# A four-layer graph-attention stack: the second projection of layer 1 as a Strassen product over two graphs, with the instruction order taken from a run of the plan

## The chip, the cores and the metric

The kernel runs on one core of a Trainium2 chip, in fp32. The metric is the device time of one execution in microseconds, given as the median of several runs. The engines are PE (matmul; PEld is its weight load), DVE (vector), ACT (scalar functions), POOL (GpSimd) and SP, which here only issues DMAs.

## The reference, cut to what matters

There are 128 graphs of 128 nodes with 512 features each and an integer adjacency matrix. Four attention layers follow each other, each inside `x = layernorm(x + layer(x, adj))`.

```python
# x: [128, 128, 512], adj: [128, 128, 128]
# layer 0: one head, no projection
# layer 1: two GAT layers, 4 heads of 256 and then one head of 512
h = elu(gat_layer(x, mask, W1, att_src1, att_dst1, b1, concat=True))   # W1: 512 x 1024
h = gat_layer(h, mask, W2, att_src2, att_dst2, b2, concat=False)       # W2: 1024 x 512
#   gat_layer: xl = x @ W; scores from xl @ a_src, xl @ a_dst; leaky_relu, mask, softmax over sources;
#   out = attn^T @ xl, plus bias
# layer 2: 8 heads of 64, projection 512 -> 512
# layer 3: scores from a projection to 32; softmax; out = elu(attn @ x)
```

The product that changes is `h @ W2`: for each graph a 128x1024 matrix times a 1024x512 matrix.

## The kernel before, in words

The function `graph(g)` (L373) lists the operations of one graph without running anything. Each entry is an `Op` (L56): its engine, an estimated duration, a closure that emits the instructions, and the buffers that it reads and writes. All 128 graphs have the same list.

The class `Pipeline` (L67) sets the order. `plan` (L71) places the list of one graph on a circular time table of `PERIOD` = 24.9 us: every operation gets a start time such that no two operations on an engine overlap modulo the period, with an assumed `LATENCY` (L30) from each engine to a reader on another one. Random shifts (`SEED`, `SPREAD`, L34) vary the priorities. `run` (L124) then starts graph g at g times the period, sorts all operations of all graphs and of the setup by these times, gives each new buffer the first slot of its kind that is free by then, and emits them in that order. Every engine works through its own queue in this fixed order; what lies between the engines are semaphores.

A graph's chain goes as follows. `x` and `adj` are loaded (L539, L540), POOL makes the masks (L546), and the scores of layer 0 are two multiply-and-sum instructions on DVE (L557). `spread` (L385) turns a column of scores into a row that lies on all partitions: a 32x32 block transposition on DVE (L389), a small DMA to device memory (L392) and a broadcast DMA back (L396). `attend` (L437) does the leaky ReLU on ACT (L446), a masked minimum on DVE with two SBUF operands (L454), the exponential on ACT (L463) and a reciprocal (L471). `turned` (L402) transposes: blocks of 32 on DVE (L407), a DMA out (L412) and a rearranging DMA in (L422, or L417 where the result is the moving operand). `mixed` (L527) multiplies the attention weights with the values (L530). `norm` (L478) is the layer norm, with the statistics on DVE, the root on POOL and the scaling on DVE or ACT.

`project` (L509) does all three projections, with its matmuls in L515: a chunk of at most 273 columns accumulates in one PSUM bank over the 128-row pieces of the weight, and ACT (L522) or DVE (L520) evicts it. For the product in question, the stationary operand is `hT` (a graph's hidden state transposed, 8 pieces of 128x128), the moving one is `w2a`, the weight with one score column for each half (2 x 257 columns):

```python
project(hT, lambda k, c: w2a[:, k, c, :], KH, C2, xl2, ["DVE", "ACT"])   # 2 chunks x 8 matmuls
```

POOL adds the bias of layer 1 (L603), the residual's bias (L585), and the residuals of layers 2 and 3 (L671, L704), each over 512 columns at a time.

The setup loads the weights by DMA, mostly from POOL's queue (`weights`, L211), and row vectors by broadcast DMAs onto 128 partitions (`rows`, L219, and `passing`, L222). It forms extra weight columns with `dot` (L276), `dot2` (L306) and `dots` (L326), and constants with a few matmuls (`ones_out`, L294; `shifts`, L318). These steps have times of their own, written by hand, and stand in the same sorted list, but their durations and dependences aren't part of the plan.

Of the kernel before, what the change touches and what calls it, by code (L numbers as in the profile page):

```python
# [3 lines left out]

# [6 lines left out]
F32 = mybir.dt.float32  # L11
# [5 lines left out]
P = 128  # L17
# [10 lines left out]
PERIOD = 24.9  # L28
LATENCY = {"PE": (0.0, 0.8), "DVE": (0.15, 1.4), "ACT": (0.1, 1.4), "POOL": (0.1, 1.4), "SP": (6.0, 6.0)}
URGENCY = 1.0  # L30
BANKS = 8

SEED, SPREAD = 17, 3.0
# [22 lines left out]
class Op:  # L56
    def __init__(self, engine, cost, emit, ins, outs, extra):
        self.engine, self.cost, self.emit, self.extra = engine, cost, emit, extra
        self.ins, self.outs = ins, outs
        self.bufs = list(dict.fromkeys([*ins, *outs]))  # L60

    def done(self, reader=None):
        own, other = LATENCY[self.engine]
        return self.cost + self.extra + (own if reader is self.engine else other)


class Pipeline:  # L67
# [3 lines left out]
    def plan(self, ops):  # L71
# [28 lines left out]
        while waiting:  # L100
# [16 lines left out]
            for q in after[k]:  # L117
                ready[q] = max(ready[q], t + op.done(ops[q].engine))
                missing[q] -= 1
                if not missing[q]:  # L120
                    waiting.append(q)
        return times

    def run(self, setup):  # L124
        times, until = self.plan(self.make(0)), {}
        graphs = [self.make(g) for g in range(self.n)]
        for k, op in enumerate(graphs[0]):
            for b in op.bufs:
                until[b] = max(until.get(b, 0.0), times[k] + op.done())
        names = list(until)  # L130
        events = [(t, -1, k, (emit, bufs)) for k, (t, emit, bufs) in enumerate(setup)]
        free = {}
        for g, ops in enumerate(graphs):
            alive = dict(zip(dict.fromkeys(b for op in ops for b in op.bufs), names))
            for k, op in enumerate(ops):
                events.append((g * PERIOD + times[k], g, k, op))
                op.ends = [(b, g * PERIOD + until[alive[b]]) for b in op.outs]
        for t, g, k, op in sorted(events, key=lambda e: e[:3]):
            emit, ends = op if g < 0 else (op.emit, op.ends)
            for b, end in ends:  # L140
                if b.slot is None:
                    slots = free.setdefault(b.tag, [])
                    b.slot = next((s for s, e in enumerate(slots) if e <= t), len(slots))
                    assert b.tag != "ps" or b.slot < BANKS, "too few banks"
                    slots[b.slot : b.slot + 1] = [end]
                    b.ap = self.place(b, g)
            emit()
# [3 lines left out]
def tile_gat_stack(  # L151
# [53 lines left out]

    setup = []

    def at(t, emit, bufs=()):
        setup.append((t, emit, bufs))

    def weights(t, shape, name, *loads, step=0.0, by=nc.gpsimd):  # L211


        tl = const.tile(shape, F32, name=name)
        for n, (part, src) in enumerate(loads):
            at(t + n * step, lambda part=part, src=src: by.dma_start(out=part(tl), in_=src))
        return tl

    def rows(t, ap, n, name, by=nc.gpsimd):  # L219
        return weights(t, [P, n], name, (lambda w: w, ap.partition_broadcast(P)), by=by)  # L220

    def passing(t, until, n, src=None):  # L222

        b = Buf("setup", [P, n])
        load = lambda: nc.gpsimd.dma_start(out=b.ap[: src.shape[0]], in_=src)
        at(t, load if src is not None else lambda: None, [(b, until)])
        return b
# [8 lines left out]
    C1, C2, CH = FH + 2, F // 2 + 1, FO + 2  # L236
    SH = H2 * CH
    C3 = SH + 2 * H2 + 2
    flat = "h f -> (h f)"
    w0d = rows(-20, w0_dst, F, "w0d", nc.scalar)  # L240
    w0s = rows(-20, w0_src, F, "w0s", nc.scalar)
    b0t = rows(-20, b0, 1, "b0t", nc.scalar)

    w1a = weights(-19, [P, KF, H1, C1], "w1a", *(
        (lambda w, b=b, k=k: w[b::4, k, :, :FH],
         w1.rearrange("(k b a) (h c) -> b k a h c", b=4, a=32, h=H1)[b, k])
        for k in range(KF) for b in range(4)
    ))
    a1 = [passing(-18, 90, HF, a.rearrange(flat).partition_broadcast(P)) for a in (a1_src, a1_dst)]
    b1t = rows(10, b1, HF, "b1t")  # L250
    b2t = rows(16, b2, F, "b2t")
    w2a = weights(18, [P, KH, 2, C2], "w2a", *(
        (lambda w, k=k: w[:, k, :, : F // 2], w2[k * P : (k + 1) * P].rearrange("p (s c) -> p s c", s=2))
        for k in range(KH)
    ))
    a2 = [passing(20, 130, F, a.rearrange(flat).partition_broadcast(P)) for a in (a2_src, a2_dst)]
    a3 = [passing(60, 230, F, a.rearrange(flat).partition_broadcast(P)) for a in (ah2, ah1)]
    fc = passing(60, 230, F, w_fc)
    ac = weights(60, [OUT, 2], "ac", *(
        (lambda w, s=s: w[:, s : s + 1], w_attn[0:1, s * OUT : (s + 1) * OUT].rearrange("u o -> o u"))  # L260
        for s in range(2)
    ))
    wha = weights(70, [P, KF, C3], "wha", *(
        (lambda w, b=b, k=k: w[b::4, k, :SH].rearrange("p (h o) -> p h o", h=H2)[:, :, :FO],
         wh.rearrange("h (k b a) o -> b k a h o", b=4, a=32)[b, k])
        for k in range(KF) for b in range(4)
    ), step=4, by=nc.sync)
    acb = [passing(140, 230, P) for _ in range(2)]
    fcp = passing(140, 230, F)
    wf = [passing(140, 230, F) for _ in range(2)]  # L270
    prod = [passing(-20, 230, F) for _ in range(2)]
    shift2 = const.tile([P, 2], F32, name="shift2")
    swf = const.tile([P, 2], F32, name="swf")
    turn = [0]

    def dot(w, a, out):  # L276

        turn[0] ^= 1
        nc.vector.tensor_tensor_reduce(
            out=prod[turn[0]].ap[:, : a.shape[1]], in0=w, in1=a, scale=1.0, scalar=0.0, op0=ALU.mult,  # L280
            op1=ALU.add, accum_out=out,
        )

    for k in range(KF):
        for s in range(2):
            for h in range(H1):
                at((31, 33, 56, 58)[k] + s + h / 4, lambda k=k, s=s, h=h: dot(
                    w1a[:, k, h, :FH], a1[s].ap[:, h * FH : (h + 1) * FH], w1a[:, k, h, FH + s : FH + s + 1]
                ))


    at(30, lambda: nc.vector.tensor_scalar_add(b1t, b1t, 1.0))

    def ones_out(s):  # L294
        pf = psum.tile([P, 512], F32, tag=f"ps{6 + s}", name=f"pc_{s}")
        for k in range(KH):
            nc.tensor.matmul(  # L297
                pf[:, : F // 2], lhsT=minus, rhs=w2a[:, k, s, : F // 2], start=(k == 0), stop=(k == KH - 1)
            )
        cols = slice(s * F // 2, (s + 1) * F // 2)  # L300
        nc.vector.tensor_add(b2t[:, cols], b2t[:, cols], pf[:, : F // 2])

    for s in range(2):
        at(44 + s, lambda s=s: ones_out(s))

    def dot2(k, s):  # L306
        turn[0] ^= 1
        nc.vector.tensor_tensor_reduce(
            out=prod[turn[0]].ap.rearrange("p (s c) -> p s c", s=2), in0=w2a[:, k, :, : F // 2],
            in1=a2[s].ap.rearrange("p (s c) -> p s c", s=2), scale=1.0, scalar=0.0, op0=ALU.mult,  # L310
            op1=ALU.add, accum_out=w2a[:, k, s, F // 2 : C2],
        )

    for k in range(KH):
        for s in range(2):
            at(100 + 3 * k + 1.5 * s, lambda k=k, s=s: dot2(k, s))

    def shifts():  # L318
        pf = psum.tile([P, 512], F32, tag="ps7", name="pc_2")
        for k in range(KH):  # L320
            nc.tensor.matmul(pf[:, :2], lhsT=minus, rhs=w2a[:, k, :, F // 2], start=(k == 0), stop=(k == KH - 1))
        nc.vector.tensor_copy(shift2, pf[:, :2])

    at(126, shifts)

    def dots(k, a, cols):  # L326

        turn[0] ^= 1
        pr = prod[turn[0]].ap.rearrange("p (h o) -> p h o", h=H2)
        nc.vector.tensor_mul(  # L330
            pr, wha[:, k, :SH].rearrange("p (h o) -> p h o", h=H2)[:, :, :FO],
            a.ap.rearrange("p (h o) -> p h o", h=H2),
        )
        nc.vector.tensor_reduce(out=wha[:, k, cols], in_=pr, op=ALU.add, axis=AX.X)

    def columns(s):

        nc.vector.tensor_copy(acb[s].ap[:OUT], ac[:, s : s + 1].to_broadcast([OUT, P]))
        pf = psum.tile([P, 512], F32, tag="ps7", name=f"pf_{s}")
# [15 lines left out]
    for s in range(2):  # L355
        at(142 + 3 * s, lambda s=s: columns(s))
# [389 lines left out]
```

## Time and profile before

| what | value |
|---|---|
| median of 3 runs | 3253.45 us (3248.8 to 3255.87) |
| the profiled execution | 3255.44 us, span 3253.7 us |
| mean granted TensorE clock | 0.977 |
| PE, DVE busy over the span | 3113.7 us, 2862.7 us |
| ACT, POOL busy over the span | 2143.7 us, 1906.0 us |
| DMA | 601.07 MB, mean 185 GB/s |

The busy times are sums over the whole span; the table of stretches tells how they lie in the beginning, the middle and the end. In a group by line, the columns are: line, engine, operation, output and input names (buffer numbers left out), shapes and count; then the group's busy time in us and the mean of one instruction in ns; then the engine's idle time just before them and who ended it. A matmul in fp32 shows as two records. Buffers that share one size have one name, `w`, so groups are told apart by line.

### The profile page before, as it was taken

What the parts mean: (1) busy time and instruction counts of PE and PEld (TensorE: products, weight loads), DVE (VectorE), ACT (ScalarE), POOL (GpSimd) and SP (SyncE); (2) the same over time, 40 slices, a digit from 0 to 9 for tenths busy, and PEclk for the clock granted to TensorE, in tenths of its full rate; (3) what the DMA queues carried; (4) which work ended last, traced back from release to release, by engine and by line L of the source; (5) the groups of instructions that cost most, each with busy time, mean ns of one, the idle gap of its engine ahead of it and who ended that gap; (6) DMA issues with size and microseconds to landing.
All of it is one profiled execution on the core that took longest, in us unless ns stands there. A gap on an engine that the chain in (4) does not pass through costs nothing.

```text
span 3253.7 us, 61851 instructions
## 1 busy us (share of the span) xinstructions
PE 3113.7 (96%) x15292; PEld 2582.4 (79%) x15292; DVE 2862.7 (88%) x10005; ACT 2143.7 (66%) x7297; POOL 1906.0 (59%) x2985
## 2 busy tenths in 40 slices
PE   4799999999999999999999999999999999999973
PEld 2578888888888888888888888888888888888852
DVE  4678999999999999999999999999999999999875
ACT  1246676766767667677676767667676676776664
POOL 5344566656666566665666666566665666656434
PEclk8899999999999999999999999999999999999985
DMA  5257778878777777777777787777777777787764
GB/s 147 79 135 180 195 187 202 193 183 207 188 198 192 193 198 187 201 189 197 196 191 198 185 204 192 191 198 187 200 191 194 197 188 199 190 199 194 171 168 105
DMA packets 1639736, 601.07 MB, mean 185 GB/s; under 512 B 1309696, under 2 KB 1489920, under 8 KB 1639376
## 3 DMA queue, kind: packets, MB, share of 16 engines
q1 hardware_dynamic: 1636608, 589.44, 73.8%
q0 software_dynamic: 2336, 7.15, 0.7%
q8 instruction: 123, 2.02, 0.3%
q14 instruction: 237, 1.94, 0.2%
q10 hardware_dynamic: 432, 0.52, 0.1%
HBM read 369.43 MB, written 227.48 MB: 183 GB/s over the span
## 4 chain that ended last, share of the span: by engine, by line
PE 93%; DVE 3%; DMA 2%; issue 1%; POOL 1%; ACT 0%; SPq 0%; POOLq 0%; DVEq 0%; ACTq 0%
PE ps L515 69%; PE ps L530 10%; PE ps L619 7%; PE ps L659 6%; DVE w L454 1%; DMA w<-row 1%; DMA w<-scr 0%; PE ps L568 0%; DVE w L407 0%; DVE st L481 0%; PE pc L297 0%; DMA w2a<-in_L_gnn_W_dram 0%; DMA w1a<-in_L_gnn_W_dram 0%; DVE w L700 0%; DVE w L557 0%
## 5 line engine op out<-in xcount | busy, mean ns | idle before, releaser
L463 ACT ACTIVATE w<-w,nm 128x128 f32<-128x128 f32 x1920 | 749.3, 392 | 432.7 <-DVE nm L454 432.7
L515 PE MATMUL ps<-w2a,w 128*128 128x257 f32 x4096 | 968.7, 384 | 10.3 <-DVE w L569 9.1
L515 PE MATMUL ps<-w1a,w 128*128 128x258 f32 x4096 | 917.6, 382 | 0.3 <-DMA w<-scr 0.3
L515 PEld LDWEIGHTS ps<-w1a,w 128*128 128x128 f32 x4096 | 779.1, 190 | 173.2 <-issue 59.5
L454 DVE CUSTOM_DVE_ANT_0 w<-w,w 128x128 f32<-128x128 f32 x1920 | 852.2, 563 | 14.2 <-ACT w L446 13.9
L515 PEld LDWEIGHTS ps<-w2a,w 128*128 128x128 f32 x4096 | 762.7, 191 | 116.1 <-DVE w L569 9.9
L522 ACT COPY xl<-ps 128x258 f32<-128x258 f32 (+2 forms) x768 | 289.7, 377 | 409.1 <-PE ps L515 393.8
L407 DVE STREAM_TRANSPOSE w<-w 128x512 f32<-128x512 f32 (+1 forms) x1024 | 547.8, 547 | 9.8 <-ACT w L463 3.0
L446 ACT ACTIVATE w<-w,xl 128x128 f32<-128x128 f32 x1536 | 474.2, 391 | 88.4 <-DMA w<-row 68.5
L515 PE MATMUL ps<-wha,w 128*128 128x273 f32 x2048 | 511.1, 396 | 13.9 <-DMA w<-scr 13.9
L515 PEld LDWEIGHTS ps<-wha,w 128*128 128x128 f32 x2048 | 381.2, 191 | 151.9 <-issue 40.8
L500 ACT ACTIVATE w<-w,mr,rd 128x512 f32<-128x512 f32 x384 | 309.0, 807 | 89.3 <-POOL mr L493 81.4
L463 ACT ACTIVATION_READ_ACCUMULATOR w<-w,nm 128x1 f32 x1920 | 362.1, 189 | 0.0
L481 DVE BATCH_NORM_STATS2 st<-w 128x6 f32<-128x512 f32 x512 | 345.0, 674 | 9.1 <-POOL w L704 2.8
L704 POOL TENSOR_TENSOR w<-w,w 128x512 f32<-128x512 f32 x128 | 163.0, 1274 | 316.6 <-DVE w L700 316.6
L486 POOL TENSOR_TENSOR rd<-rd,neghalf 128x1 f32<-128x1 f32 x512 | 322.8, 630 | 42.6
L659 PEld LDWEIGHTS ps<-xl,w 128*128 128x128 f32 x2048 | 273.7, 195 | 88.6 <-issue 69.2
L603 POOL TENSOR_TENSOR xl<-xl,b1t 128x512 f32<-128x512 f32 x256 | 312.6, 1241 | 0.0
L485 POOL TENSOR_SCALAR rd<-mv 128x1 f32<-128x1 f32 x512 | 115.9, 226 | 332.4 <-DVE mv L482 304.0
L530 PE MATMUL ps<-w,w 128*128 128x512 f32 x512 | 278.3, 626 | 26.9 <-DMA w<-scr 9.9
L671 POOL TENSOR_TENSOR w<-z,w 128x512 f32<-128x512 f32 x128 | 151.4, 1183 | 243.6 <-PE ps L515 135.8
L454 DVE DVE_READ_ACCUMULATOR2_ANT nm<- 128x1 f32 x1920 | 292.3, 152 | 0.0
(98 smaller groups left out, 3900.4 us busy)
## 6 DMA issues: line engine op xcount, KB each, us to landing
scr<-w SPq DMA_DIRECT2D x640, 256.0 KB
w<-scr SPq DMA_DIRECT2D x640, 256.0 KB
w<-row SPq DMA_DIRECT2D x128, 512.0 KB
w<-in_x_dram SPq DMA_DIRECT2D x128, 256.0 KB
w<-row SPq DMA_DIRECT2D x128, 256.0 KB
out_dram<-w SPq DMA_DIRECT2D x128, 256.0 KB
w<-row SPq DMA_DIRECT2D x384, 64.0 KB
scr<-w SPq DMA_DIRECT2D x384, 64.0 KB
```

Of the source, the lines that this page charges most:

```text
L407: op("DVE", 0.12 + 0.133 * n, lambda: nc.vector.transpose(zb.ap.rearrange("p b h c -> p h b c"), src.ap.rearrange("p (h b c) -> p h b c", ...
L446: nc.scalar.activation(z.ap[:, h, :], db.ap[:, h0 + h, :], AF.Prelu, bias=src(h0 + h), alpha=SLOPE)
L454: nc.vector.tensor_tensor_reduce(out=zz.ap[:, h, :].rearrange("p (b a) -> p a b", b=4), in0=z.ap[:, h, :].rearrange("p (a b) -> p a b", b= ...
L463: nc.scalar.activation(zz.ap[:, h, :], zz.ap[:, h, :], AF.Exp, bias=nm.ap[:, h : h + 1], scale=-1.0, accum_out=rs.ap[:, h : h + 1],)
L481: op("DVE", 0.6, lambda: nc.vector.bn_stats(st.ap, y.ap), [y], [st])
L486: nc.gpsimd.tensor_tensor(out=rd.ap, in0=rd.ap, in1=neghalf, op=ALU.pow)
L500: op("ACT", 0.6, lambda: nc.scalar.activation(y.ap, y.ap, AF.Identity, bias=mr.ap, scale=rd.ap), [y, rd, mr], [y])
L515: op("PE", w * 4 / 2400 + 0.006, lambda k=k: nc.tensor.matmul(px.ap[:, :w], lhsT=lhs.ap[:, k, :], rhs=wa(k, c), start=(k == 0), stop=(k == ...
L522: op("ACT", 0.06 + w / 1200, lambda: nc.scalar.copy(dst(), px.ap[:, :w]), [px], [t])
L530: op("PE", width * 4 / 2400, lambda: nc.tensor.matmul(pa.ap[:, :width] if len(xv.shape) == 2 else pa.ap.rearrange("p (s c) -> p s c", s=2) ...
L603: op("POOL", 1.3, lambda h=h: nc.gpsimd.tensor_add(xl.ap[:, h : h + 2, :FH], xl.ap[:, h : h + 2, :FH], b1t[:, h * FH : (h + 2) * FH].rearr ...
L659: op("PE", 0.225, lambda u=u, h=h: nc.tensor.matmul(pa.ap[:, u * CH : (u + 1) * CH], lhsT=pt.ap[:, u, :], rhs=xl3.ap[:, h * CH : (h + 1) * ...
```

## The change

Three things change at once.

**The product over two graphs.** `hT @ W2` of graphs 2n and 2n+1 is one product of 2 x 2 blocks: the rows are the two graphs, the inner dimension is split into two halves of 512, the columns into two halves of 257. A Strassen product (in Winograd's form) needs seven block products in place of eight. The weight `w2s` holds seven blocks: four of the weight and three formed once in the setup from differences. The new function `halves` lists the operations. For an odd graph it forms two sums of `hT` blocks on POOL, and multiplies four of the products; in the following graph's list come the other three, with two more sums. The partial results are kept by accumulating further products into the same PSUM bank, by copies to SBUF on ACT (`taken`) and by additions of PSUM and SBUF on DVE (`added`). The plan knows one averaged list (`graph(None)`), in which the part after the product waits two periods (`op.wait`); a last list for g = 128 carries only the second part of the last pair.

**The order.** `plan` still gives times, now for `PERIOD` 28.0 and longer latencies. A new `order` goes through all operations with one clock for each engine and shorter latencies (`FLOW`): it always takes the operation that could start first, among those whose planned time is at most `AHEAD` = 30 us beyond the earliest one not yet issued, and gives out buffer slots as they come free in this run. The number of slots still comes from the plan.

**The loads as operations.** The setup's steps are `Op`s with durations, inputs and outputs, so `order` places them too. Row vectors are loaded as one row, and a matmul with ones spreads them (`spread_row`). The first weight comes from the ACT and SP queues in eight DMAs of each, the second from POOL's queue in four.

Besides, the mask of layer 3 is no longer kept from the start: the adjacency is loaded again in the third part. A graph's list is split into `first`, `second`, `halves` and `third`, which otherwise hold what was there.

```diff
-PERIOD = 24.9
-LATENCY = {"PE": (0.0, 0.8), "DVE": (0.15, 1.4), "ACT": (0.1, 1.4), "POOL": (0.1, 1.4), "SP": (6.0, 6.0)}
-URGENCY = 1.0
+PERIOD = 28.0
+LATENCY = {"PE": (0.0, 0.8), "DVE": (0.15, 1.6), "ACT": (0.1, 1.6), "POOL": (0.1, 1.6), "SP": (6.8, 6.8)}
+FLOW = {"PE": (0.0, 0.6), "DVE": (0.15, 0.9), "ACT": (0.1, 0.9), "POOL": (0.1, 0.9), "SP": (4.5, 4.5)}
+AHEAD = 30.0
+URGENCY = 0.3
...
-SEED, SPREAD = 17, 3.0
+SEED, SPREAD = 1, 8.0
...
+    def order(self, events):
...
+        while len(out) < n:
+            best = None
+            for e, waiting in known.items():
+                found = None
+                for i in waiting:
+                    if events[i][0] > events[low][0] + AHEAD and i != low:
+                        break
+                    t = start(i)
+                    if t is not None and (found is None or t < found[0]):
+                        found = (t, i)
+                        if t <= clock[e]:
+                            break
+                if found and (best is None or found < best):
+                    best = found
...
+    def spread_row(t, r, a):
+
+        b = passing(512, "ps")
+        at(t, "PE", 0.86, lambda: nc.tensor.matmul(
+            b.ap, lhsT=ones[0:1, :], rhs=r.ap[0:1, a : a + 512], start=True, stop=True
+        ), [r], [b])
+        return b
...
+    at(109, "POOL", 2.5, lambda: nc.gpsimd.tensor_sub(w2s[:, 5], w2s[:, 2], w2s[:, 3]), [summed_up], [t3])
+    at(109.1, "DVE", 1.1, lambda: nc.vector.tensor_sub(w2s[:, 3], w2s[:, 3], w2s[:, 0]), [summed_up, t3], [t1])
+    at(109.2, "DVE", 1.1, lambda: nc.vector.tensor_sub(w2s[:, 4], w2s[:, 2], w2s[:, 3]), [t1], [t2])
+    at(109.3, "DVE", 1.1, lambda: nc.vector.tensor_sub(w2s[:, 6], w2s[:, 1], w2s[:, 4]), [t2], [t4])
...
-        xl2 = Buf("xl2", [P, 2, C2])
-        project(hT, lambda k, c: w2a[:, k, c, :], KH, C2, xl2, ["DVE", "ACT"])
...
+            a11, a12, a21, a22 = (part(h, a) for h in ("h0", "h1") for a in range(2))
+            do((0, 1), "POOL", 1.27, {
+                1: summed(ALU.add, "s1", a21, a22), 0: summed(ALU.subtract, "s3", a11, a21), None: None
+            }, {"t": ["h1"], 1: ["h1"], 0: ["h0", "h1"]}, {"t": ["s1"], 1: ["s1"], 0: ["s3"]})
+            do((0, 1), "POOL", 1.27, {
+                1: summed(ALU.subtract, "s2", whole("s1"), a11), 0: summed(ALU.subtract, "s4", a12, whole("s2")), None: None
+            }, {"t": ["h1", "s1"], 1: ["s1", "h0"], 0: ["h0", "s2"]}, {"t": ["s2"], 1: ["s2"], 0: ["s4"]})
...
+            product((1,), ("h1", "q1"), {1: ("pa", "h0", a11, 0, True)})
+            taken((1,), ("q1", "t1"), {1: ("pa", "t1")})
+            product((0, 1), ("s1", "q2"), {1: ("pc", "h0", a12, 1, True), 0: ("pa", "s3", whole("s3"), 5, False)})
+            added((0, 1), ("q2", "t1"), {1: ("pc", "t1", "xl0", 0), 0: ("pa", "v", "xl1", 1)})
+            taken((0,), ("q2", "u3"), {0: ("pa", "u3")})
+            product((0, 1), ("s2", "q3"), {1: ("pb", "s1", whole("s1"), 3, True), 0: ("pb", "s4", whole("s4"), 2, False)})
+            taken((1,), ("q3", "v"), {1: ("pb", "v")})
+            added((0,), ("q3",), {0: ("pb", "u2", "xl0", 1)})
+            product((0, 1), ("s2", "q4"), {1: ("pa", "s2", whole("s2"), 4, False), 0: ("pd", "h1", a22, 6, True)})
+            taken((1,), ("q4", "u2"), {1: ("pa", "u2")})
+            added((0,), ("q4", "u3"), {0: ("pd", "u3", "xl1", 0)})
...
+            at, m3 = Buf("adj", [P, P], I32), Buf("m3", [P, P])
+            op("SP", 0.4, lambda: nc.sync.dma_start(out=at.ap, in_=adj[g]), [z3], [at], 1.0)
+            mask(m3, at, ALU.is_equal)
```

In `product`, each name stands for four matmuls of 128x257 over the four pieces of its operand, accumulating in the named bank; the number is the block of `w2s`, and the last entry tells whether the bank starts anew.

## The prediction

> **What bounds the kernel now.** I read three views in this order: the busy times by engine, the table of stretches, and the groups by line for the middle of the run. The first says which engine could be the bound, the second where it is.
>
> ```profile
> PE 3113.7 (96%) x15292; PEld 2582.4 (79%) x15292; DVE 2862.7 (88%) x10005; ACT 2143.7 (66%) x7297; POOL 1906.0 (59%) x2985
> ```
> ```profile
> core 0: us, PE busy (x) PEld busy (x) DVE busy (x) ACT busy (x) POOL busy (x), PEclk, DMA share, GB/s
> ...
> 20.00:40.00 20.00, 10.80 (x35) 8.35 (x35) 10.69 (x45) 0.40 (x1) 7.07 (x10) 1.00 0.51 167
> 40.00:60.00 20.00, 7.85 (x22) 5.36 (x23) 13.67 (x55) 1.39 (x5) 8.52 (x14) 0.66 0.39 99
> ...
> 1000.00:2000.00 1000.00, 1000.00 (x4993) 835.31 (x4992) 920.52 (x3233) 701.61 (x2393) 616.26 (x966) 1.00 0.79 194
> ```
> In the stretch from 1000 to 2000 us PE has no gap at all: 1000 of 1000 us busy, at full clock. DVE is at 92%, ACT 70%, POOL 62%. The chain of waits has PE on 93% of the span. One group with one record for each graph (the 128x257 eviction) appears 42 times, and the chain repeats the same piece every 23.84 us (1495.88, 1519.72, 1543.56), so a graph costs 23.84 us there. All the 140 us in which PE is idle lie before 200 us (71) and after 3000 us (69). So the middle is bound by PE, the ends by the latency of a graph's own chain.
>
> ```profile
> L515 PE MATMUL ps<-w2a,w 128*128 128x257 f32 x1344 | 314.5, 381 | 0.0
> L520 DVE COPY xl<-ps 128x257 f32<-128x257 f32 x42 | 16.9, 403 | 0.0
> L663 DVE TENSOR_TENSOR z<-ps,ri 128x264 f32<-128x264 f32 x84 | 35.4, 421 | 0.0
> L454 DVE CUSTOM_DVE_ANT_0 w<-w,w 128x128 f32<-128x128 f32 x630 | 284.6, 572 | 0.0
> L603 POOL TENSOR_TENSOR xl<-xl,b1t 128x512 f32<-128x512 f32 x84 | 102.6, 1241 | 0.0
> ```
> The first row is the product that changes: 32 records a graph (two for each of its 16 matmuls), 314.5 / 42 = 7.49 us. The fourth has a mean of 572 ns although its median over the run is 381. The order of time shows why:
>
> ```profile
> 1498.85 2.44 POOL L603 TENSOR_TENSOR xl<-xl,b1t 128x512 f32<-128x512 f32 x2
> 1499.01 1.34 DVE L454 CUSTOM_DVE_ANT_0 w<-w,w 128x128 f32<-128x128 f32 x1
> ...
> 1500.20 1.34 DVE L454 CUSTOM_DVE_ANT_0 w<-w,w 128x128 f32<-128x128 f32 x1
> ...
> 1501.39 0.38 DVE L454 CUSTOM_DVE_ANT_0 w<-w,w 128x128 f32<-128x128 f32 x1
> ```
> A masked minimum takes 1.34 us while a POOL addition of 512 columns runs, and 0.38 when it is over: 0.96 us lost each time. Over the stretch that is 630 x (0.572 - 0.381) = 120 us, or 2.87 us a graph (three such hits). Without them DVE needs (920.5 - 120) / 42 = 19.06 us a graph.
>
> **What the skill says.** The Trainium skill's "SBUF — State Buffer", section "SBUF: two separate sides", says that GpSimd and a DVE instruction with two SBUF inputs take one shared port pair as an exclusive lock for the whole instruction. The trace agrees: L454 has two SBUF inputs and waits out L603. Its "Perfetto Trace Analysis", section "Identifying the Most-Contended Engine", warns that busy matmul time is a poor measure and asks for weight-load time as well; that is 84% here, so I trust "PE bound" from the missing gaps, not from the 96%. Its "DMA: Bandwidth & Descriptors", section "Issuing engines are not separate DMA queues", says that DMAs of all engines share the same 16 and only issue time is saved by another queue; no run here shows it yet.
>
> **The change part by part.**
>
> *The product.* Sixteen matmuls a graph become 28 for two graphs. The listing of instructions shows 1792 in the new product line and 3072 in the other projections, against 5120 before in one line: 256 fewer. At 2 x 234 ns each (314.5 us / 1344 = 234 ns a record) that is 0.94 us a graph, so PE needs 22.90 us. In the fully busy stretch, 200 to 3040 us, there are 2840 / 23.84 = 119 graphs: **-111 us**. The remaining nine graphs' saving falls where PE waits anyway, and I count it at nothing.
>
> *DVE.* One 257-column copy a graph (0.40 us) becomes two additions of PSUM and SBUF; the nearest row is the 264-column product, 0.42 us. That is +0.44, so 19.50 us a graph before blocking.
>
> *POOL.* Four 512-column additions for two graphs, at 1.24 to 1.28 us (L603, L704): +2.5 us a graph, 14.7 becomes 17.2 of 22.9. POOL's own time is hidden; what it costs is the lock. In the new order, each graph's eight masked minima of layer 2 (DVE) stand right behind the ELU, while POOL's queue has there the last addition of layer 3 and then an operand sum, with nothing between but short instructions. I expect one or two hits of up to 1 us there. The two bias additions come directly behind the layer-2 residual now, while DVE has some 4 us of statistics, transposes and scaling to do, so their two hits should mostly go. I put the blocked time at 3.3 us a graph (between 2 and 5.8: two and six hits of 0.96 among eight large POOL operations, for three of six now). DVE then needs 22.8 us, 0.1 below PE.
>
> *ACT.* The 257-column eviction (375 ns) goes from one to two a graph: 17.1 of 22.9 us. The work beside it hides that; it is on the path only once per pair, through PSUM bank reuse.
>
> *PSUM.* Two banks of the pair stay occupied from one graph into the next, and their copies have to end before accumulation goes on in the same bank. The matmuls that stand between (other projections and head products, several us) cover a copy of 0.4 us. If DVE falls behind, this cover is what goes first.
>
> *SP and the DMAs.* The adjacency is loaded a second time, for layer 3, so its mask needn't be held: +128 DMAs of 64 KB, 8.4 on 589 MB. The SP queue's entries from 1499.4 to 1523.2 us add up to 20.2 of 23.8 us; with one more (0.3 to 0.7) it is 20.7 of 22.9, 90%. The DMA share goes from 79% to about 79 x 1.014 x 23.84 / 22.9 = 83%. One place is tighter: the layer-2 writes of the transposed heads and their reads now stand five rows apart on SP for many graphs, where ten stood before, so SP waits for the landing there and queues the loads behind it. Hidden as long as SP doesn't reach 100%.
>
> *The order.* The plan's times are run through per-engine queues, and an operation may be put up to 30 us ahead. The stretch that has no gap can't gain from it. The price is between zero and some tenths of a us a graph: with PE at 22.9 and DVE at 22.8 in one fixed order, any lateness of DVE shows as a bubble on PE. I take 0.15 x 119 = **+18 us** (0 to 0.5, so 0 to 60).
>
> *Head.* Row vectors come as 2 to 4 KB and are spread by 13 matmuls (about 1 us each, into idle PE) in place of about 3.3 MB of broadcast DMAs. In the head above, the first operand transposition left at 21.5 us and the first large matmul of layer 1 began at 54.5, with three DMA round trips of 7 to 9 us in between beside that traffic. One graph more may start early. But the third layer starts two periods later, so PE has less to do. I take **-10** (-40 to +20).
>
> *Tail.* Once the last hidden state is there, two sums (2.5 us) and 20 of the pair's 28 matmuls are left, 9.4 us against 7.5 for 16; that is 4.4 more, and with a hop between engines **+5** (0 to 15). After that, two graphs do layer 2 side by side rather than one after the other, at no cost, since from 3140 us on PE is idle over half.
>
> *Sum.* The profiled execution took 3255.4 us (span 3253.7), 2 above the median 3253.45. 3255.4 - 111 + 18 - 10 + 5 = 3157; less 2, **3155 us** as the median.
>
> **The rivals.**
>
> *DVE becomes the bound, mildly.* For it: 92% busy already, and 22.8 against 22.9 is within my error. Against: it needs blocked time over 3.4 us. At 3.9 a graph costs 23.4, a saving of 0.44 x 119 = 52; with head and tail about 3197.
>
> *The port lock takes it all back (slower).* Every added POOL sum meets a two-input DVE instruction, and the later work on DVE meets more of the old ones. It decides from 23.84 - 19.50 = 4.34 us of blocked time a graph. With six hits it is 5.8, a graph costs 25.3, and the time is 3255 + 1.46 x 119 = about 3425. For it: POOL rises from 62% to 75% busy. Against: PE, not DVE, sets the pace now, and the two structural hits go.
>
> *SP or the DMAs become late (slower).* If the waits of write-then-read add 3.5 us to SP's 20.7, a graph costs 24.2: +43, about 3300. Against: nine rows or more stand between most pairs, as now.
>
> *The ends gain more.* If starting graphs early and the missing broadcasts fill 40 us of the 71 in the head, and PE shows no bubbles, the time is 3255 - 111 - 40 = about 3105.
>
> *The change doesn't save what it says.* The listing has the 256 matmuls gone, of one shape; this one has no share.
>
> **How the numbers follow.** A measurement here can tell 0.2%, 6.5 us, from no change. The main case (3120 to 3185) has 0.43, the mild DVE bound 0.22, the good ends 0.13: together 0.78 faster. Within 0.2% falls 0.05, between the mild case and the two rivals on the other side. Slower has 0.17: the lock 0.12, SP 0.05. The range, 3098 to 3265, takes in the three fast cases and the near edge of those two.
>
> **What would show it.** Right: PE still without gaps in the middle, a period near 23.05 us, DVE at 97 to 99%, the masked minimum's mean still near 600 ns, POOL near 75%. Wrong: a period above 23.3 with DVE at 100% and a masked mean above 650 ns (the lock); PE waiting for DMA landings with SP full (the queue); or PE idle of over 150 us at the ends. A period of 22.9 with no idle would say that my bubble was invented.

## The result, and the profile after

The changed kernel takes 3279.78 us (median of 5 runs, 3269.54 to 3289.32), 1.0081 times the time before, with a 95% interval of 1.0055 to 1.0107. It is slower by 0.8%; 3155 us was forecast. Its profiled execution took 3273.89 us, with a span of 3272.1.

First the busy times by engine, then the stretch from 1000 to 2000 us, both of the kernel after:

```profile
PE 3072.9 (94%) x14822; PEld 2483.6 (76%) x14822; DVE 2939.1 (90%) x10185; ACT 2157.7 (66%) x7427; POOL 2259.4 (69%) x3211
```
```profile
1000.00:2000.00 1000.00, 964.15 (x4737) 784.28 (x4736) 919.24 (x3219) 692.71 (x2389) 725.04 (x1032) 1.00 0.79 194
```
TensorE, which had no gap in this stretch, now is idle for 35.9 us of it, and no other engine is full: DVE 92%, POOL 73%. One transposition in each graph (L844) starts at 1004.79 and, 41 graphs later, at 1998.74: the period is **24.24 us** a graph, where it was 23.84 and 23.05 was forecast. So a graph has 964.15 / 41.25 = 23.37 us of busy TensorE and 0.87 us of idle.

The head, by the table of stretches (the first columns are TensorE's busy time and records):

```profile
20.00:40.00 20.00, 13.06 (x38) 8.83 (x36) 17.20 (x80) 0.90 (x3) 3.46 (x6) 0.96 0.10 27
40.00:60.00 20.00, 12.29 (x19) 5.56 (x20) 14.35 (x66) 1.30 (x4) 3.80 (x6) 0.50 0.42 96
...
0.00:200.00 200.00, 160.80 (x579) 116.93 (x580) 150.58 (x459) 52.43 (x173) 83.73 (x100) 0.84 0.40 107
3040.00:3272.00 232.00, 164.08 (x715) 124.67 (x713) 176.74 (x619) 142.36 (x473) 121.51 (x208) 0.80 0.66 162
```
Up to 200 us TensorE is idle for 39 us, where it was 71; after 3040 us for 68, where it was 69. So the head gains and the tail does not lose.

What TensorE waits for, and the groups of matmuls that the waits stand ahead of, same stretch (busy us, mean ns of one, idle us before them):

```profile
PE ps L704 <- DMA w<-scr: 29.7, 34, 3.0
```
```profile
L704 PE MATMUL ps<-wha,w 128*128 128x273 f32 x663 | 168.6, 399 | 28.4 <-DMA w<-scr 27.5 <-ACT w L635 0.8
L788 PE MATMUL ps<-w2s,w 128*128 128x257 f32 x1158 | 282.0, 382 | 0.0
L643 DVE CUSTOM_DVE_ANT_0 w<-w,w 128x128 f32<-128x128 f32 x616 | 265.8, 533 | 7.4 <-PE ps L719 4.3 <-ACT w L635 2.6 <-DMA scr<-w 0.3
```
Most of the idle time, 27.5 of 35.9 us, is one wait. The projection of layer 2 (weights `wha`) waits for its transposed operand to come back from DRAM (`w<-scr`). The product itself (L788) waits for nothing, and the masked minimum (L643), which I feared, has a shorter mean than before (572).

The order of time on SP, the queue that issues these read-backs. Before (columns: start, us, line, what, how many in a row):

```profile
1504.44 1.91 SPq L422 DMA_DIRECT2D w<-scr  x2
...
1510.32 1.15 SPq L422 DMA_DIRECT2D w<-scr  x2
...
1516.12 0.41 SPq L422 DMA_DIRECT2D w<-scr  x1
...
1522.53 0.63 SPq L422 DMA_DIRECT2D w<-scr  x1
```
After:

```profile
1506.93 0.43 SPq L585 DMA_DIRECT2D w<-row  x1
1507.45 7.39 SPq L611 DMA_DIRECT2D w<-scr  x3
1514.89 1.91 SPq L601 DMA_DIRECT2D scr<-w  x2
```
The three read-backs by themselves (least, median and longest in ns), and what TensorE does then:

```profile
L611 SPq DMA_DIRECT2D w<-scr x3: 634/1130/5431, 1507.4 to 1513.7; - x3
```
```profile
1514.97 0.70 PE L704 MATMUL ps<-wha,w 128*128 128x273 f32 x2 [1.46 <-DMA w<-scr]
```
The new order puts three read-backs of 256 KB in a row, 41 times in the stretch, once a graph. A single one takes SP about 0.65 us to issue. On three in a row SP stands for 4.9 to 7.4 us, and the one shown is the longest; a broadcast of 512 KB is just ahead of them. Here the first takes 0.63 us, the second 5.43 and the third 1.13. Added up over the stretch, SP's DMA issues take 21.2 us a graph after (18.4 before), and those of `w<-scr` 8.3 (5.2 before). SP is at 87%, not full.

TensorE's matmuls on their operand begin at 1514.97. That operand is the first of the three (e9 below tells the kinds apart). So its own issue was short, and it landed about 7.5 us after it: from 1507.45 to 1514.97. That SP comes free at the same moment, at 1514.89, is not what TensorE waited for.

### The profile page after: what moved, and what is told of

Same layout as the page of the kernel before. It is cut to its first block, busy times and chain, and to the rows that moved or that the text cites. A ratio compares the mean times of both kernels' runs of the same rounds, so it can differ in the third digit from the quotient of the medians.

```text
span 3272.1 us, 62627 instructions
## 1 busy us (share of the span) xinstructions
PE 3072.9 (94%) x14822; PEld 2483.6 (76%) x14822; DVE 2939.1 (90%) x10185; ACT 2157.7 (66%) x7427; POOL 2259.4 (69%) x3211
## 4 chain that ended last, share of the span: by engine, by line
DVE 32%; PE 24%; DMA 19%; ACT 7%; POOL 6%; issue 6%; SPq 1%; POOLq 0%; DVEq 0%; ACTq 0%
PE ps L704 14%; DVE w L643 12%; DMA w<-scr 8%; DMA scr<-w 6%; DVE w L596 6%; PE ps L788 5%; DVE st L670 3%; ACT w L652 3%; DMA w<-row 2%; ACT w L635 2%; PE ps L719 2%; DMA w<-in_x_dram 2%; PE ps L932 2%; DVE w L727 2%; PE ps L890 2%
## 5 line engine op out<-in xcount | busy, mean ns | idle before, releaser
L704 PE MATMUL ps<-w1s,w 128*128 128x258 f32 x4096 | 930.6, 385 | 21.7 <-DMA w<-scr 13.1
L704 PEld LDWEIGHTS ps<-w1s,w 128*128 128x128 f32 x4096 | 779.0, 192 | 191.6 <-DVE z L936 18.7
L788 PE MATMUL ps<-w2s,w 128*128 128x257 f32 x3584 | 873.8, 383 | 10.0 <-POOL w L774 9.6
L643 DVE CUSTOM_DVE_ANT_0 w<-w,w 128x128 f32<-128x128 f32 x1920 | 841.2, 538 | 33.5 <-ACT w L635 16.2
L788 PEld LDWEIGHTS ps<-w2s,w 128*128 128x128 f32 x3584 | 657.3, 191 | 122.2 <-issue 27.4
L704 PE MATMUL ps<-wha,w 128*128 128x273 f32 x2048 | 522.5, 402 | 75.6 <-DMA w<-scr 66.5
L674 POOL TENSOR_SCALAR rd<-mv 128x1 f32<-128x1 f32 x512 | 143.0, 279 | 432.2 <-DVE mv L671 310.8
L675 POOL TENSOR_TENSOR rd<-rd,neghalf 128x1 f32<-128x1 f32 x512 | 345.8, 675 | 42.7
L635 ACT ACTIVATE w<-w,sc 128x128 f32<-128x128 f32 x384 | 151.4, 396 | 297.2 <-DMA scr<-w 237.6
L643 DVE DVE_READ_ACCUMULATOR2_ANT nm<- 128x1 f32 x1920 | 287.2, 150 | 0.0
L932 PE MATMUL ps<-xl,w 128*128 128x66 f32 x2048 | 256.1, 274 | 18.6 <-DMA w<-scr 16.5
```

The source lines that it names most:

```text
L635: nc.scalar.activation(z.ap[:, h, :], db.ap[:, h0 + h, :], AF.Prelu, bias=src(h0 + h), alpha=SLOPE)
L643: nc.vector.tensor_tensor_reduce(out=zz.ap[:, h, :].rearrange("p (b a) -> p a b", b=4), in0=z.ap[:, h, :].rearrange("p (a b) -> p a b", b= ...
L675: nc.gpsimd.tensor_tensor(out=rd.ap, in0=rd.ap, in1=neghalf, op=ALU.pow)
L704: op("PE", w * 4 / 2400 + 0.006, lambda k=k: nc.tensor.matmul(px.ap[:, :w], lhsT=lhs.ap[:, k, :], rhs=wa(k, c), start=(k == 0), stop=(k == ...
L788: return lambda: nc.tensor.matmul(q[b].ap[:, :C2], lhsT=x()[:, k, :], rhs=w2s[:, slot, k, :], start=(fresh and k == 0), stop=(k == 3), ski ...
L932: op("PE", 0.225, lambda u=u, h=h: nc.tensor.matmul(pa.ap[:, u * CH : (u + 1) * CH], lhsT=pt.ap[:, u, :], rhs=xl3.ap[:, h * CH : (h + 1) * ...
```

## The experiments

All ratios are to the kernel before, with 95% intervals; the changed kernel stands at 1.0081. Periods are worked out from the table of the same stretch: matmul records divided by 119 a graph without the Strassen product, 115 with it.

### Which part of the change costs

**e1_plan_order** keeps product and loads, and takes the order directly from the plan's times, as before; the plan's own numbers had to be others to fit.

```
-PERIOD = 28.0   SEED, SPREAD = 1, 8.0    order: run of the plan, AHEAD = 30
+PERIOD = 26.0   SEED, SPREAD = 469, 8.0  order: events sorted by planned time
```


> The Strassen product with the setup as operations, but emitted in the order of the plan's times as the kernel before does it, with no run of the plan (period 26.0, the latencies of before, a seed whose buffers fit the memory). Theory A (the order puts DMA reads too late for PE: it assumes 4.5 us for a load, and three large read-backs stand in a row on SP): PE is without gaps again, a graph costs 22.9 to 23.3 us, 3140 to 3190 us in all. Theory B (the added POOL sums block DVE through the shared port): no change against the changed kernel, 3260 to 3290. Theory C (the product itself stalls PE, by its banks and copies): also 3260 to 3290, with PE waiting in the product's line.

Measured: 3388.7 us, 1.0416 [1.0401, 1.0432]. From 4707 records the period is 24.4 us, so the middle is no better, and the ends are worse. None of the three theories had this time. In the stretch TensorE waits only 4.6 us for landings, but 31.0 us for DVE's product of layer 2's heads (L861 of this run), which reads them out of PSUM; 24.3 us of that stand ahead of the Strassen product. That is the sign of theory C, in this order alone. So taking the new order away removes one wait and brings another.

**e2_order_only** leaves the Strassen product out and keeps the new order and the loads.

```
-        xl2 = halves(hT)
+        project(hT, lambda k, c: w2s[:, SLOT[k // 4, c], k % 4, :], KH, C2, xl2, ["DVE", "ACT"], ...)
```


> The new order and the loads as operations alone: each graph's product is 16 plain matmuls again, with no sums, no pairs and no wait of two periods. A: PE shows gaps at loads as in the changed kernel, 0.5 to 1.4 us a graph over 23.84, so 3310 to 3430 us. B and C: as the kernel before, 3230 to 3270, since nothing of the product is left.

Measured: 3265.31 us, 1.0045 [1.0029, 1.0061].

```profile
1000.00:2000.00 1000.00, 990.80 (x4911) 820.07 (x4910) 844.59 (x3178) 678.13 (x2348) 625.29 (x949) 1.00 0.77 193
```
That is 1000 x 119 / 4911 = 24.23 us a graph, the same period as with the product, although each graph has two matmuls more. But TensorE is 99.1% busy here: 24.01 us of the 24.23 are work, 0.17 more than before, and 0.22 are idle. SP stands for up to 7.67 us on three read-backs here too, and yet TensorE waits for landings for only 7.3 us of the stretch, against 29.7. Why its own work takes longer stays open.

**e3_longer_flow** changes one number of the run of the plan: what it takes a DMA to last.

```
-FLOW = {... "SP": (4.5, 4.5)}
+FLOW = {... "SP": (6.8, 6.8)}
```


> The changed kernel, with one number changed: the run of the plan assumes 6.8 us instead of 4.5 for a DMA (FLOW of SP). A: PE's queue puts the projections later, the gaps before the layer-2 projection shrink, 3170 to 3250 us. B and C: no change, 3260 to 3290. If the memory is what holds the chain short, no change either.

Measured: 3456.45 us, 1.0625 [1.0604, 1.0647], 25.6 us a graph. TensorE waits for POOL's mask (L732) instead, 58.3 us of the stretch. With a more careful duration for every DMA the order came out worse.

### Is another unit the bound?

**e4_no_sums** (the four POOL sums are not issued), **e7_smaller_store** (a quarter of the output's columns stored) and **e8_no_second_adj** (the second load of the adjacency not issued) keep the order and take work away. **e5_before_more_bytes** and **e6_before_one_issue** add work to the kernel before.

```
e4 -  return lambda: nc.gpsimd.tensor_tensor(out=q[o].ap, in0=a(), in1=b(), op=what)
e4 +  return lambda: None
e7 -  nc.sync.dma_start(out=out[g], in_=y.ap)
e7 +  nc.sync.dma_start(out=out[g, :, 0:P], in_=y.ap[:, 0:P])
e8 -  op("SP", 0.4, lambda: nc.sync.dma_start(out=at.ap, in_=adj[g]), [z3], [at], 1.0)
e8 +  op("SP", 0.4, lambda: None, [z3], [at], 1.0)
e5 +  nc.scalar.dma_start(out=spare, in_=x[g])
e6 +  nc.sync.dma_start(out=spare, in_=x[g, 0:1, 0:4])
```


> The changed kernel in the same order on every engine, but the four POOL sums of a pair are not issued, and the products that read them take a constant 128x128 matrix instead, so the product is not the reference's. A: DVE gets 0.5 to 1 us a graph back, but PE still waits for the same loads: 3230 to 3280 us. B: DVE is the pacemaker, so the time falls by what the lock cost: 3140 to 3190.

> The kernel before, with one more load of 256 KB a graph into a tile that nothing reads, issued from ACT's queue. Theory D (the DMAs have a floor of their own: every variant so far moved 191 to 194 GB/s in the middle, and the kernel before stood at this floor and at PE's at once): 4.62 MB a graph become 4.88, the period goes from 23.84 to about 25.2 us, 3410 us in all, and PE gets gaps. Theory A (no floor; only the order of the changed kernel makes loads late): PE stays without gaps, 3250 to 3275 us.

> The kernel before, with one more DMA of 16 bytes a graph on SP's queue into a tile that nothing reads: an issue without bytes. D: no change, 3245 to 3265 us. If SP's issuing is the floor (some 20 of 23.8 us): +0.4 to 0.9 us a graph, 3300 to 3365. A: no change.

> The changed kernel, which stores only 128 of the 512 columns of each result, so the output isn't the reference's: 192 KB a graph less on the DMAs, on no chain that a graph waits for. D: 4.71 MB become 4.52, the period goes from 24.27 to 23.3 us, 3150 to 3180 us. A: somewhat shorter queues, 3240 to 3280.

> The changed kernel in the same order, but the second load of the adjacency isn't issued, and the mask of layer 3 is computed from a constant, so the output isn't the reference's: 64 KB and one issue on SP a graph less. D: the period falls by 1.4%, 0.33 us, so 3235 to 3250 us. If SP's issuing is the floor: 0.4 to 0.7 us, 3190 to 3235. A: 3260 to 3285.

Measured: e4 3314.27 us, 1.0182 [1.0155, 1.0209]; e5 3254.32, 1.0006 [0.9998, 1.0015]; e6 3251.79, 0.9997 [0.9988, 1.0005]; e7 3273.6, 1.0055 [1.0037, 1.0073]; e8 3297.32, 1.0129 [1.0108, 1.0151]. e4 in the same stretch:

```profile
1000.00:2000.00 1000.00, 952.97 (x4674) 772.09 (x4673) 849.47 (x3177) 672.93 (x2357) 609.66 (x933) 1.00 0.78 191
```
Without the sums, POOL falls from 725 to 610 us and DVE, which they block, from 919 to 849 (the mean of a masked minimum from 533 to 423 ns); the period still rises to 24.6. The port lock is real, but it isn't the bound in this order. e7, with 192 KB a graph less, can't be told from the changed kernel, and e8, with one DMA fewer, is slower. The kernel before takes 256 KB a graph and one issue a graph more at no cost, so neither the bytes nor the number of issues was short in it. I read e5 too broadly at this point: it added long rows on another engine's queue, and says nothing on many short pieces in a burst.

### Buffers, or the order?

**e9_own_buffers** keeps the order and gives the large read-backs places of their own; **e10_more_slots** and **e11_order_more_slots** run the order again with more places, with and without the product.

```
e9  +  b.tag, b.slot = "w512" + b.own, n % {...}[b.own]   # two of each of three kinds, by turns
e10 +  more = {"w512": 5, "w128": 6, ...}             # and w2s cut to its four blocks
e11 +  more = {"w512": 6, "w128": 12, "xl3": 1, "xl2": 1, "adj": 1, "ae": 1, ...}
```


> The changed kernel with its order kept instruction for instruction. The read-backs of four parts that are not scaled (layer 1's and layer 2's turned output and the heads) land in buffers of their own, two of each kind by turns, and no longer in those that every 128x512 tile shares. To pay for the memory, the three differences of the weights and the sum that joins them are not formed and the seven products read the four blocks as they are (left out: that part of the result). Theory E (a read-back waits for a shared buffer that comes free late, then takes 6 to 7 us to land, and TensorE waits for it): SP's waits for the scalar engine ahead of L611 fall, TensorE's wait for landings falls from 3% to under 1%, and the middle goes from 24.3 to under 23.8 us a graph: under 3215 us, ratio below 0.98. Rival F (the order itself, which puts writes and reads a few places apart whatever the buffers): same within 0.3%, with the same wait of TensorE for landings.

> The changed kernel with the same memory taken from the weights (the same part of the result left out), and the order run again with five more 128x512 slots, six more 128x128 slots and one or two more of each small kind. Theory E: with more places free the run of the plan puts read-backs earlier, period under 23.8 us a graph, under 3215 us. Rival F: the plan's chain of steps is what the order follows and it takes the slots without getting shorter; within 1% of the changed kernel, 3250 to 3310 us.

> Without the Strassen product, with the new order and the loads as operations (as in e2), and with the memory that the weights' sums don't take given to the order as slots: six more 128x512, twelve more 128x128, one more of each two-graph kind, one or two more of the small kinds. Theory E: the middle returns to TensorE's 23.84 us a graph and the ends keep what the new order gained (some 36 us): 3217 us, faster than both kernels. Rival F: 24.2 us a graph as in e2 and 3265 us.

Measured: e9 3332.33 us, 1.0239 [1.0221, 1.0257]; e10 3343.1, 1.0275 [1.0250, 1.0300]; e11 3244.41, 0.9970 [0.9962, 0.9978]. SP in e9:

```profile
1505.38 0.73 SPq L619 DMA_DIRECT2D w512b<-scr  x1
1506.57 4.80 SPq L619 DMA_DIRECT2D w512c<-scr  x2
```
```profile
PE ps L712 <- DMA w512b<-scr: 29.3, 31, 1.8
```
`w512b` is the operand of layer 2's projection, `w512c` are the heads of layer 2. The burst is still there, with the buffers no longer shared, and TensorE waits for its first read-back as before; for those of the heads it doesn't wait. The Trainium skill's "Perfetto Trace Analysis", section "Optimization Strategy", says that the same gap coming again and again can mean too little SBUF or PSUM. I followed that, and e9 and e10 give it no support. They don't exclude it cleanly: two places for two head read-backs a graph may themselves be tight. e11 gained 0.7% on e2. In its trace SP's longest stand on read-backs is 3.8 us against 7.7, so its order has smaller bursts. The places as such can't be credited: e16, below, has them too and is slower than e2.

**e12_other_seed**, **e15_seed45** and **e16_order_38** draw another order from the same planner: the first two of the changed kernel, the third of e11.

```
-SEED, SPREAD = 1, 8.0
+SEED, SPREAD = 38, 8.0     # e12, e16;   45 in e15
```


> The changed kernel with one number changed: the seed of the plan's random shifts, 38 for 1 (same operations, a plan that also fits the memory with 1.5 KB more). Theory F (the period comes from the particular order): the time moves by tenths of a per cent up to two per cent in either direction, 3220 to 3340 us, and TensorE's wait for landings moves with it. If the floor were a unit or the memory alone, it stays within 0.3% of 3280 us.

> The changed kernel with seed 45 in place of 1 (a plan that takes exactly the same memory). Theory F: somewhere between e12's 3243 and 3340 us, not within 0.3% of 3280. If e12 was better only by its memory: within 0.3% of 3280 us.

> As e11 (no Strassen product, new order, more slots) with seed 38. It tells what the product is worth when the order is drawn anew. Theory F: within 1% of e11's 3244 us to either side, TensorE over 99% busy in the middle. If a good order is worth more than the product: under 3225 us, faster than every kernel so far.

Measured: e12 3243.55 us, 0.9971 [0.9959, 0.9983]; e15 3239.81, 0.9962 [0.9947, 0.9977]; e16 3282.53, 1.0094 [1.0077, 1.0111]. The same change with another seed beats the kernel before. One number that computes nothing moves the time by 1.2%, more than the change as a whole. e15 has the lowest median of the kernels that leave nothing of the computation out, but can't be told from e12 and e11.

The bursts alone don't tell a good order from a bad one. In e15 SP stands for up to 7.77 us on three read-backs, and TensorE waits for landings for 15.2 us of the stretch. In e16 SP never stands longer than 1.75 us on a read-back and in e10 never longer than 2.93 us on one or two in a row, and TensorE still waits 16.4 and 44.4 us.

### What in the order is late?

**e13_landed** takes the wait of each read-back for its write away, **e14_small_broadcast** most bytes of the broadcasts of four and eight heads, **e17_long_pieces** the short pieces of the read-backs, **e18_light_dma** the last two together. All keep the changed kernel's order.

```
e13 -  flat = lambda: scr.ap.rearrange("p f -> (p f)")
e13 +  flat = lambda: w1.rearrange("p f -> (p f)")[g % 8 * 4 * P * P :][0 : n * P * P]
e14 -  in_=row.ap.rearrange("h j -> (h j)").partition_broadcast(P)
e14 +  in_=row.ap[0].partition_broadcast(P)
e17 -  in_=flat().rearrange("(q p h c) -> p h q c", q=4, p=P, h=n)     # 128 bytes a piece
e17 +  in_=flat().rearrange("(q p e) -> p q e", q=4, p=P)              # 512 bytes a piece
```


> The changed kernel, same order and same instructions; every read-back of a transposition reads a part of the weights in DRAM in place of what was just written (left out: the transposed values, so the output differs from the reference's). The writes stay. No read-back waits for its write any more. Theory G (the round trip through DRAM, write and then read, is what comes late for TensorE): SP's waits for scr disappear, TensorE's wait for landings falls under 0.5%, the middle goes to 23.3 us a graph: about 3170 us. Rival F (the order of the queues; the round trip is one of many steps of a chain that runs over DVE, ACT and POOL too): a gain of at most 1%, 3245 to 3285 us.

> The changed kernel, same order; each broadcast of a row of logits brings only the first head's row, and all heads use that (left out: the other heads' own destination terms). Broadcasts of four heads move a quarter of their bytes. Theory G in its second form (the read-backs land late, after 6 to 7 us, because the broadcasts are ahead of them in the DMA engines): the large read-backs land within 3 to 4 us, DMA share falls from 0.79 to about 0.6, the middle goes under 23.8 us a graph: under 3215 us. Rival F: the landings get shorter, but the time stays within 1% of 3280 us.

> The changed kernel, same order; the read-backs of four parts read pieces of 512 bytes in place of 128, same bytes, same buffers, with no change to those who use them (left out: the right arrangement of the transposed values). Theory H (three large read-backs in a row, of many short pieces, block SP for 6 to 7 us and land late, and the fixed order has no slack for it): SP's longest issue falls from 7.4 to under 3 us, TensorE's wait for landings goes, the middle goes to 23.5 us a graph: about 3190 us. If it is the bytes or the order alone: within 1% of 3280 us.

> e14 and e17 together: broadcasts of one head's row and read-backs in pieces of 512 bytes (the same parts of the result left out). Theory H: with both, no read-back is late, TensorE sets the pace at 23.2 to 23.4 us a graph, and with the ends of the changed kernel the time is 3140 to 3170 us, near the forecast. If DVE, at 96% in e14, is next: no more than 0.5% under e14's 3206 us.

Measured: e13 3246.91 us, 0.9987 [0.9980, 0.9994]; e14 3205.66, 0.9861 [0.9846, 0.9875]; e17 3206.8, 0.9859 [0.9842, 0.9875]; e18 3200.57, 0.9839 [0.9824, 0.9853].

e13: the wait for the write isn't the main thing. SP still stands on the three, though nothing they read is fresh:

```profile
1518.30 6.48 SPq L611 DMA_DIRECT2D w<-in_L_gnn_W_dram  x3
```
e17, same bytes, same order, same buffers. The packets (first after, then e17), then e17's stretch, its waits of TensorE and SP's burst:

```profile
DMA packets 1657571, 606.13 MB, mean 185 GB/s; under 512 B 1311562, under 2 KB 1508170, under 8 KB 1657204
```
```profile
DMA packets 871139, 606.13 MB, mean 189 GB/s; under 512 B 262986, under 2 KB 721738, under 8 KB 870772
```
```profile
1000.00:2000.00 1000.00, 983.83 (x4876) 808.56 (x4875) 956.57 (x3310) 709.09 (x2455) 750.16 (x1060) 1.00 0.68 200
```
```profile
PE ps L844 <- POOL w L732: 15.7, 40, 0.7
PE ps L704 <- DMA w<-scr: 0.4, 1, 0.4
```
```profile
1521.78 2.72 SPq L611 DMA_DIRECT2D w<-scr  x3
...
1545.81 3.61 SPq L611 DMA_DIRECT2D w<-scr  x3
```
```profile
L611 SPq DMA_DIRECT2D w<-scr x3: 359/455/559, 1521.8 to 1524.1; - x3
```
```profile
1530.52 0.62 PE L704 MATMUL ps<-wha,w 128*128 128x273 f32 x2
```
TensorE's wait for landings goes from 29.7 us to 0.4, the DMA share from 0.79 to 0.68 with the same 606 MB moved, and the period from 24.24 to 23.60 (L844 at 1012.75 and, 41 graphs on, at 1980.41). 0.64 x 119 graphs is 76 us; the time fell by 73. The Trainium skill's "DMA: Bandwidth & Descriptors", section "Why small descriptors are slow (HBM only)", says that each packet carries a fixed overhead that weighs on short ones; the fall in the share agrees.

What has changed for SP is more than the share says. None of the three read-backs holds it longer than 0.56 us now; what is left of the 2.72 us is waiting between them. Its issues take 16.3 us a graph in place of 21.2. The operand itself doesn't land sooner after its issue. By the semaphores in the traces, the first of the three lands after 6.3 us in the median (6.1 in the changed kernel). But TensorE takes it up later after the issue, 7.6 us in the median against 6.2; here it is 8.74 us, from 1521.78 to 1530.52, without a wait. So SP, held up less, issues it earlier.

In e14, too, TensorE has no wait for landings left; this is all that its list of waits shows in the stretch:

```profile
PE ps L844 <- POOL w L732: 16.6, 42, 0.7
```
SP still stands 4.2 to 5.9 us on the three, but the first of them lands after 4.8 us in the median. So the two remedies act in different places, and either is enough: with long pieces the read-back is issued earlier, with small broadcasts it lands sooner. What was late in this order is **a read-back of short pieces, the first of three, right behind a large broadcast**. That it is three in a row wasn't tried by itself: no run sets them apart and leaves pieces and broadcasts as they are. Both remedies also take load off the DMA engines everywhere (shares of 0.68 and 0.73), and so a part of the gain can come from other places than the burst. e18 adds nothing much to either (0.2%), so the 3140 to 3170 us of theory H did not come; its stretch has DVE at 95.7% like theirs. From there on, transfers aren't the bound.

What is left of TensorE's idle time, 0.38 us a graph, is a transposition (L844) that waits for POOL's mask (L732). The added POOL sums don't stand ahead of that mask: in each of the 42 graphs of e17's stretch, POOL first pauses for 1.4 or 2.3 us ahead of the layer norm's small steps (L674), and the twelve instructions from there to the mask hold none of the sums. Whether the sums make that start late by way of DVE wasn't tried.

## Why the prediction was wrong

**The step that failed** is the hiding of SP and the DMAs: "Hidden as long as SP doesn't reach 100%." SP is at 87% and the DMA share at 0.79, and a transfer is late in most graphs all the same: 29.7 us of waits in 41.25 graphs, 0.72 us a graph, where I had put this at nothing. I used averages over the period for something that happens within 7 us of it. I had even seen the place from the order: writes and reads of the transposed heads closer together on SP. But I thought only of the wait for the write. Taking that away is worth 1% (e13); longer pieces for the same reads are worth 2.2% (e17).

The figure for SP, 20.7 us a graph, was near the measured 21.2 by luck. My 20.2 for the kernel before took in a row of the next period (the broadcast at 1523.20, 1.39 us); one period's rows add up to 18.8. The change added 2.8 us a graph, not 0.5. The rival "SP or the DMAs become late", with 24.2 us a graph and about 3300 us, came nearest; it had 0.05. Its 24.2 is luck too, since it had SP full.

**Point by point**, against the forecast of 3157 us for the profiled execution, in the stretch of 119 graphs:

- *Order's bubble.* 0.15 us a graph forecast (18 us), 0.87 measured: +86 us. In e17, 0.49 of it (0.87 - 0.38) goes with the late read-backs; 0.38 stays, as the wait for the mask.
- *The product.* The matmuls went as listed, 28 records a graph in place of 32. But a record of the product takes 282.0 / 1158 = 243.5 ns, not 234, so the saving is 7.49 - 6.82 = 0.67 us a graph and not 0.94: +32 us. This is the mis-sized term of the saving. e17 has 243.6 without any late transfer, so it isn't the lateness. Nor is it the new order: as plain products in orders drawn that way the same shape takes 227.5 to 229.1 ns (e11, e2, e16), and with the Strassen product and its sums 235.6 to 244.4 in every order drawn here (e3 and e15 at the ends). So the longer record goes with the Strassen form; what in it costs the time stays open. With 0.2 us more in other groups, TensorE needs 23.37 where I had 22.90.
- *DVE.* 919.24 / 41.25 = 22.3 us a graph, 22.8 forecast. The masked minimum's mean fell to 533 ns, where I had about 600, and no saturation came of the lock.
- *POOL, ACT.* POOL 17.6 us (17.2 forecast), ACT 16.8 (17.1). e4 refutes the port lock as the bound.
- *PSUM.* L788 shows no idle time before it; the cover held.
- *Ends.* -5 forecast in sum. The span grew by 18.4 us and the middle by 0.40 x 119 = 48, so the ends gave back 29. TensorE idles 32 us less in the head and about as long in the tail, so the head was right in direction and too small (10), and the tail's 5 did not show. e2 shows it without the product: its middle is 0.39 us a graph slower, 46 us, and its span only 4.8 us longer.

The sum: 1.19 us a graph over 23.05, times 119, is 141; less 24 at the ends is 117, the distance from 3157 to 3273.9.

So the matmuls' saving was real, and about seven tenths of what I counted. With transfers that arrive in time (e17) the kernel is 1.4% faster than before. As it was drawn, the order spent the saving and more on waits, most of them for read-backs.

## What to carry to other kernels

A queue that is 87% full can still be late. Before calling its transfers hidden, find the one that an engine will wait for, see in the order of time what stands ahead of it, and compare the time from its issue to its landing with the time until its use. Count a read in short pieces by its pieces, not its bytes. When an order is drawn anew, part of the result belongs to the draw: run a second seed before putting the time down to the change.

## What the runs showed that I had not expected

- Taking work away from a fixed order made it slower: 1.0% without POOL's sums (e4), 0.5% without one load (e8), against the changed kernel. Why their period rises wasn't settled.
- The same 256 KB read-back holds the issuing queue for about 0.65 us alone or as the first of three, and for 3.0 to 5.4 us as the second. In pieces of 512 bytes the second takes 0.4 to 0.7 us.
- With the transfers in time (e17) the pattern locks: pairs of graphs come nearly alike, about 23.2 and 24.0 us in turn. In the changed kernel the spacing of the same transposition (L844) wanders between 23.2 and 26.9 us.
